# Gate rows on ScalarE and GpSimd, the output weight let go ahead of them, the binarized weight two steps later, in an adaLN Mamba-2 block

## The chip, the core and the metric

The kernel runs on one NeuronCore of a Trainium2 chip, in float32 throughout. The metric is the device time of one execution in microseconds (us), the median of several runs. The work is spread by hand over five engines: TensorE (PE in the profile: matmul and transpose; its weight loads are shown apart as PEld), VectorE (DVE), ScalarE (ACT), GpSimd (POOL) and SyncE (SP). SP does no arithmetic here, it issues transfers (DMAs). Each engine works through its own list of instructions strictly in order; an instruction that waits for another engine holds up everything behind it in its list. This is as true of SP's DMAs as of a matmul.

## The reference, cut to what matters

Four sequences of 512 tokens, 512 features each, go through two residual blocks. Six vectors per sequence, from one small product, shift, scale and gate them:

```python
mod = (silu(c) @ wmod).reshape(4, 6, 1, 512)
sa, ca, ga, sb, cb, gb = mod[:, 0] ... mod[:, 5]
ga = (2 * (ga >= 0) - 1) * maximum(abs(ga), 0.25)
gb = (2 * (gb >= 0) - 1) * maximum(abs(gb), 0.25)
h = layernorm(x) * (1 + ca) + sa
x = x + ga * mamba(h)          # in_proj, conv of 4 taps, silu, chunked scan, out_proj
h = layernorm(x) * (1 + cb) + sb
x = x + gb * (h @ bw.T + bias) # bw = sign(w) * mean(abs(w), row), 512 x 512
```

The Mamba part has 64 heads of width 16, 8 groups with state size 64, and chunks of 128 tokens. The change touches how `ga`, `gb` and `gb * bias` are made and when, and when `bw` is made.

## The kernel before, in words

**Tiles.** The 2048 tokens are cut into 8 halves `h` of 256 tokens, each into 2 chunks `c` of 128. A unit is one pair of the eight groups in one chunk, so a half has 8 units and the kernel 32, numbered u0, u1, ... here. Unit u is finished in step u by `stage2` (L630).

**A half's front.** `f_norm` (L307) normalizes the tokens on VectorE, with a power on GpSimd in it (`rs`, L298). `f_hT` (L335) turns them on TensorE (L330) and scales them on ScalarE (L347); its first columns are zeroed on GpSimd (L340). `f_dt` makes the step sizes, a long chain of small VectorE instructions (L371 to L404) that starts from the product `pa` (L368). `conv_pair` (L440) does two projections of 128 columns (`proj`, L434), and the convolution: one ScalarE instruction (L450) and three VectorE taps (L454) for each. A projection's PSUM bank is free when its last tap has read it; the pool `ps` has five such banks (tag "mm").

**A unit.** `stage0` (L570) has SP load the running sums that the decays come from (L541, L542) into one of two pairs of tiles, free when `py` of the unit two before has read it. ScalarE does 16 exponentials (L549), VectorE multiplies by the masked products (L625), TensorE forms `py` (L212, L215) and `stage2` gates it on VectorE and GpSimd.

**A chunk's tail.** `tail1` (L729) multiplies by the output weight `wout` (`po`, L739) and applies `gates`, `tail2` (L751) turns and modulates, `tail3` (L765) multiplies by the binarized weight `bwT` (`pf`, L775). For the first chunk they are in steps 4, 5 and 7.

**What is done once, in the first steps.** `load_late` (L181, step 0) loads the weights of four of the six vectors into places that are not yet in use: `wout`, `bwT`, two tiles of tag "z" and two thirds of `room`, the tile of tag "gates". `late_mods` (L233, step 1) multiplies them (`pg`), turns two of the rows for the second block, and makes the gates from the other two: five VectorE instructions (L256 to L260) on tiles of tags "h2" and "th", one load of the bias (L255) and three writes to DRAM (L262), all four on SP. `load_wout` (L264, step 2) can only load the 2 MB of the output weight when the products have read what lay there. `load_gates` (L717, step 3) reads the rows back, spread over 128 partitions. `signs(o)` (L269; two in step 2 and two in step 3) loads 128 rows of the second block's weight (L272), forms its row means (`alpha`, L274), signs (L277) and their product (L278, ScalarE). `turned_signs(o)` (L281; two in step 5, two in step 6) turns them on TensorE (L285) and puts them in `bwT` (L286).

**What sets the order.** The functions are called step by step, in each step those of the list `steps` (filled at L814 to L837) in the order of filling, then the unit's `burst`, `stage2`, `stage0` and `stage1`. A planner then fixes each engine's list before the run: by a model of times it takes what it holds to be ready, the earlier in the program first. Tiles of one tag share a fixed number of places ("h2" 2, "th" 2, "C" and "B" 3 each, "t" and "gates" 1): the first instruction that writes a tile waits until a place is free. `behind` (L781) puts a step's TensorE instructions behind the newest projection.

Of the kernel before, what the change touches and what calls it, by code (L numbers as in the profile page):

```python
# [11 lines left out]
F32 = mybir.dt.float32  # L12
AF = mybir.ActivationFunctionType
ALU = mybir.AluOpType
# [4 lines left out]
B, L, DM = 4, 512, 512  # L19
# [21 lines left out]
def adaln_mamba_block(  # L41
# [15 lines left out]
    nc = tc.nc  # L57
# [13 lines left out]
    wk = ctx.enter_context(tc.tile_pool(name="wk", bufs=2))  # L71
# [47 lines left out]
    gate_d = dram.tile([B, 3, DM], F32, name="gate_d")  # L119
# [25 lines left out]
    def load_wm_at(t6, place, k0=0):  # L145

        n = place.shape[1]
        nc.sync.dma_start(place, wm_v[:, k0 : k0 + n, t6 * DM : (t6 + 1) * DM])
        for k in range(n):
            wms[t6, k0 + k] = place[:, k]  # L150
# [27 lines left out]
    room = wk.tile([P, 3, DM], F32, tag="gates", name="wm3_g", bufs=1)  # L178
    room_z = wm_tiles(3, "z", 6, 2)

    def load_late(h):  # L181

        load_wm_at(2, wout[:, 0:NK])
        load_wm_at(5, wout[:, NK:])
        load_wm_at(4, bwT)
        for k in range(2):
            load_wm_at(3, room_z[k].unsqueeze(1), k)
        load_wm_at(3, room[:, 0:2, :], 2)


    sc = keep.tile([P, NK, 32], F32, name="sc")
# [17 lines left out]
    def glued(products, after=None):  # L209

        with tc.issue_after(after) if after else nullcontext():
            first = products[0]()  # L212
        with tc.issue_after(first.ins), tc.high_priority(offset=1000):
            for product in products[1:]:
                product()  # L215
# [17 lines left out]
    def late_mods(h):  # L233

        pg = ps.tile([P, DM], F32, tag="mm", name="pg")
        glued([
            partial(
                mm, pg[32 * j : 32 * j + 32, :], sc[:, k, :], wms[t6, k], start=(k == 0), stop=(k == NK - 1)
            )
            for k in range(NK) for j, t6 in enumerate((2, 5, 4, 3))  # L240
        ])
        row = wk.tile([P, DM], F32, tag="t", name="rows", bufs=1)
        nc.vector.tensor_copy(row, pg)
        pm = ps.tile([P, NK, P], F32, tag="mm", name="pm")
        for dt in range(NK):
            nc.tensor.transpose(pm[:, dt, :], row[:, dt * P : (dt + 1) * P], ident)
        nc.vector.tensor_copy(modT[:, 2], pm[:, :, 96 : 96 + B])
        nc.vector.tensor_scalar(modT[:, 3], pm[:, :, 64 : 64 + B], 1.0, None, ALU.add)

        g = row[0:64, :]  # L250
        sg = wk.tile([64, DM], F32, tag="h2", name="sg")
        ab = wk.tile([64, DM], F32, tag="h2", name="ab")
        brow = wk.tile([64, DM], F32, tag="th", name="brow")
        second = slice(32, 32 + B)
        nc.sync.dma_start(brow[second, :], ffn_b.partition_broadcast(B))  # L255
        nc.vector.tensor_scalar(sg, g, 0.0, 2.0, ALU.is_ge, ALU.mult)  # L256
        nc.vector.scalar_tensor_tensor(ab, g, -1.0, g, ALU.mult, ALU.max)
        nc.vector.tensor_scalar(ab, ab, 0.25, None, ALU.max)
        nc.vector.scalar_tensor_tensor(sg, sg, -1.0, ab, ALU.add, ALU.mult)
        nc.vector.tensor_mul(ab[second, :], sg[second, :], brow[second, :])  # L260
        for i, v in enumerate((sg[0:B, :], sg[second, :], ab[second, :])):
            nc.sync.dma_start(gate_d[:, i, :], v)  # L262

    def load_wout():  # L264
        nc.sync.dma_start(wout, w_outT.rearrange("(k p) e -> p k e", p=P))
# [548 lines left out]
    def at(step, f, *args):  # L814
        steps.setdefault(step, []).append((f, args))

    for h in range(NHALF):
        for step, f, args in (FIRST, SECOND)[h] if h < 2 else FRONT:
            at(max(0, h - 1) * NU + step, f, h, *args)
        if h % HPB == 0:  # L820
            at(h * NU + 3, load_gates, h // HPB)
        if h == 0:
            at(0, load_late, h)
            at(1, behind, 0, late_mods)
            at(2, load_wout)
            for o in range(NK):
                at(o // 2 + 2, signs, o)
    for o in range(NK):
        at(o // 2 + 5, behind, 1, turned_signs, o)
    for h in range(NHALF):  # L830
        for c in range(2):
            end = h * NU + (c + 1) * NP
# [7 lines left out]
    h = NHALF - 1  # L840
# [65 lines left out]
```

## Time and profile before

| what | value |
|---|---|
| median of 3 runs | 736.16 us (735.45 to 738.33) |
| the profiled execution | 737.38 us |
| its span, first to last instruction | 735.7 us |
| TensorE busy | 700.4 us, 95% of the span |
| VectorE busy | 599.5 us, 81% |
| ScalarE busy | 522.0 us, 71% |
| GpSimd busy | 254.8 us, 35% |
| TensorE clock granted, mean | 0.993 of full |

A busy share is a mean over the span. The chain of work that ended last is followed back from the last instruction, at each step to what released it. A timeline lists instructions of one engine with start and length; idle time stands in brackets with what ended it. A table of windows gives each engine's busy time in stretches of the span, with TensorE's granted clock, the share of the DMA engines and their rate.

### The profile page before, as it was taken

The numbers are of one execution on the slowest core, as the hardware profiler recorded it, in microseconds if no ns is written. First come the engines' busy times: TensorE is split into PE (matmuls) and PEld (weight loads), VectorE is DVE, ScalarE is ACT, GpSimd is POOL, SyncE is SP. The second block draws the span as 40 slices with busy tenths as digits, with TensorE's granted clock in tenths as the row PEclk, the third lists the DMA queues.
The fourth block names the chain that finished last, engine by engine and source line by source line (L and its number), as shares of the span: only waits on it lengthen the run. The fifth ranks groups of instructions, "written<-read, shape, count | busy, mean of one in ns | idle before, by whom it ended". The sixth has DMA issues, their size and how long they took to land.

```text
span 735.7 us, 15007 instructions
## 1 busy us (share of the span) xinstructions
PE 700.4 (95%) x5196; PEld 500.8 (68%) x5196; DVE 599.5 (81%) x1170; ACT 522.0 (71%) x1507; POOL 254.8 (35%) x297
## 2 busy tenths in 40 slices
PE   6999979899999999999999999999999999999997
PEld 3786746666677666677677666776667866677754
DVE  3869888876998678986899768996799867996995
ACT  2467658748696697785976787865968768788941
POOL 4021323444243332343223342433414332333652
PEclk9999989999999999999999999999999999999999
DMA  8991693535555256444644256552564537457720
GB/s 279 328 291 41 204 208 85 135 98 142 127 132 144 63 155 137 102 115 102 159 116 130 53 116 168 142 137 53 140 132 114 130 86 176 116 150 151 142 69 29
DMA packets 119067, 99.24 MB, mean 135 GB/s; under 512 B 73984, under 2 KB 97152, under 8 KB 118992
## 3 DMA queue, kind: packets, MB, share of 16 engines
q1 hardware_dynamic: 117808, 96.39, 52.3%
q0 software_dynamic: 896, 1.38, 0.7%
q8 instruction: 41, 0.67, 0.4%
q10 hardware_dynamic: 288, 0.52, 0.2%
q14 instruction: 34, 0.28, 0.1%
HBM read 92.47 MB, written 5.79 MB: 134 GB/s over the span
## 4 chain that ended last, share of the span: by engine, by line
PE 65%; ACT 16%; DVE 9%; DMA 4%; issue 4%; POOL 1%; SPq 1%; ACTq 0%; DVEq 0%; POOLq 0%
PE po L739 14%; PE pp_x L434 11%; PE pp_z L434 10%; ACT decay L549 9%; PE pp_C L434 7%; PE pp_B L434 5%; PE pf L775 3%; PE py L212 2%; PE py L215 2%; DVE decay L625 2%; ACT h L759 2%; DVE u_x L454 2%; DMA fw<-in_ffn_w 2%; ACT win L549 2%; PE gy L215 2%
## 5 line engine op out<-in xcount | busy, mean ns | idle before, releaser
L549 ACT ACTIVATE decay<-decay,st 128x128 f32<-128x128 f32 x960 | 293.9, 395 | 4.2 <-DMA decay<-sums_d 3.7
L625 DVE SCALAR_TENSOR_TENSOR decay<-decay,gm 128x1024 f32<-128x1024 f32 x120 | 160.8, 1341 | 50.3 <-ACT decay L549 47.2
L434 PE MATMUL pp_x<-hT,win 128*128 128x259 f32 x512 | 120.7, 390 | 7.3 <-DVE u_C L454 7.3
L434 PE MATMUL pp_z<-hT,win 128*128 128x256 f32 x512 | 118.1, 383 | 0.0
L434 PEld LDWEIGHTS pp_x<-hT,win 128*128 128x128 f32 x512 | 96.9, 193 | 25.2 <-ACT decay L549 7.7
L739 PE MATMUL po<-wout,z 128*128 128x512 f32 x256 | 113.8, 595 | 0.0
L434 PEld LDWEIGHTS pp_z<-hT,win 128*128 128x128 f32 x512 | 94.3, 189 | 16.3 <-issue 3.5
L675 POOL TENSOR_TENSOR z<-yt,z 128x256 f32<-128x256 f32 x62 | 62.9, 1015 | 76.1 <-DVE yt L674 57.8
L454 DVE SCALAR_TENSOR_TENSOR u_x<-pp_x,cw,u_x 128x256 f32<-128x256 f32 x192 | 83.6, 474 | 1.3 <-ACT u_x L450 0.7
L739 PEld LDWEIGHTS po<-wout,z 128*128 128x128 f32 x256 | 47.5, 190 | 53.1 <-issue 52.4
L672 POOL TENSOR_TENSOR yt<-yt,xs 128x256 f32<-128x256 f32 x46 | 41.4, 899 | 106.3 <-DVE yt L671 78.6
L507 POOL TENSOR_TENSOR xs<-u_x,rr 128x512 f32<-128x512 f32 x32 | 42.7, 1334 | 79.2 <-DVE u_x L459 61.3
L516 ACT ACTIVATE uz<-pp_z,zb 128x256 f32<-128x256 f32 x64 | 27.5, 470 | 59.0 <-PE pp_z L434 59.0
L215 PE MATMUL py<-decay,xpad 128*32 128x128 f32 x1680 | 66.3, 276 | 0.0
L434 PE MATMUL pp_B<-hT,win 128*128 128x259 f32 x256 | 63.5, 396 | 2.7 <-ACT decay L549 1.9
L434 PE MATMUL pp_C<-hT,win 128*128 128x259 f32 x256 | 59.6, 384 | 1.1 <-DVE u_x L454 1.1
L775 PE MATMUL pf<-bwT,h 128*128 128x512 f32 (+1 forms) x136 | 59.0, 578 | 1.4 <-ACT h L759 1.3
L434 PEld LDWEIGHTS pp_B<-hT,win 128*128 128x128 f32 x256 | 47.4, 193 | 14.5 <-ACT decay L549 3.1
L450 ACT ACTIVATE u_x<-pp_x,cb,cw 128x256 f32<-128x256 f32 x64 | 35.3, 560 | 30.5 <-PE pp_x L434 30.4
L434 PEld LDWEIGHTS pp_C<-hT,win 128*128 128x128 f32 x256 | 47.8, 189 | 9.4 <-PE pn L424 1.4
L679 POOL TENSOR_TENSOR xd<-xpad,st 128x256 f32<-128x256 f32 x48 | 34.1, 727 | 55.8 <-PE pst L215 28.3
L212 PE MATMUL py<-decay,xpad 128*32 128x128 f32 x240 | 47.4, 279 | 3.2 <-issue 2.2
(157 smaller groups left out, 1080.9 us busy)
## 6 DMA issues: line engine op xcount, KB each, us to landing
decay<-sums_d SPq DMA_DIRECT2D x120, 256.0 KB
decay<-sums_d SPq DMA_DIRECT2D x120, 128.0 KB
rr<-r_d SPq DMA_DIRECT2D x64, 128.0 KB
e<-e_d SPq DMA_DIRECT2D x96, 64.0 KB
win<-in_w_inT SPq DMA_DIRECT2D x4, 1024.0 KB
xr<-in_x SPq DMA_DIRECT2D x16, 256.0 KB
res<-o SPq DMA_DIRECT2D x15, 256.0 KB
x<-in_x SPq DMA_DIRECT2D x14, 256.0 KB
```

The source lines that it names most:

```text
L212: first = products[0]()
L215: product()
L434: last = mm(pm, win[:, k, col : col + P], H[h]["hT"][:, k, lo:], start=(k == 0), stop=(k == NK - 1))
L450: nc.scalar.activation(u[:, j, :], pm[:, KS - 1 :], AF.Identity, bias=cb[:, t : t + 1], scale=cw[:, t, KS - 1 : KS])
L454: nc.vector.scalar_tensor_tensor(u[:, j, :], pm[:, k : k + T], cw[:, t, k : k + 1], u[:, j, :], ALU.mult, ALU.add)
L507: nc.gpsimd.tensor_tensor(xs, xc, rr, ALU.mult)
L549: nc.scalar.activation(ets[r][:, i, :], ets[r][:, i, :], AF.Exp, bias=H[h]["st"][:, hd : hd + 1], scale=-1.0)
L625: nc.vector.scalar_tensor_tensor(ets[r], ets[r], 1.0, bc_mid(gm[:, r, :], HPG), ALU.min, ALU.mult)
L672: ew.tensor_add(t, t, xs)
L675: ew.tensor_mul(zg, t, zg)
L739: last_po = mm(po, H[h]["z"][g // 2][:, g % 2, c * CH : (c + 1) * CH], wout[:, g, :], start=(g == 0), stop=(g == NKI - 1))
L775: mm(pf, h2[:, k, :], bwT[:, k, cols], start=(k == 0), stop=(k == NK - 1))
```

## The change

The gates leave `late_mods` for a function of their own, `late_gates`, in step 2, after `load_wout` in the list of that step. It has one VectorE instruction (signs as +-0.5), one on ScalarE (the absolute value) and three on GpSimd; the three writes are issued by GpSimd instead of SP. Its three tiles are now the thirds of `room`, and the bias is loaded at the end of `load_late`, in step 0. `signs` moves from steps 2 and 3 to steps 4 and 5, `turned_signs` from steps 5 and 6 to 6 and 7. The arithmetic is the same: sign times 0.5 times 2 times the larger of the absolute value and 0.25.

```diff
@@ in load_late @@
         load_wm_at(3, room[:, 0:2, :], 2)
+        nc.sync.dma_start(brow[second, :], ffn_b.partition_broadcast(B))
@@ in late_mods @@
         nc.vector.tensor_scalar(modT[:, 3], pm[:, :, 64 : 64 + B], 1.0, None, ALU.add)
-
-        g = row[0:64, :]
-        sg = wk.tile([64, DM], F32, tag="h2", name="sg")
-        ab = wk.tile([64, DM], F32, tag="h2", name="ab")
-        brow = wk.tile([64, DM], F32, tag="th", name="brow")
-        second = slice(32, 32 + B)
-        nc.sync.dma_start(brow[second, :], ffn_b.partition_broadcast(B))
-        nc.vector.tensor_scalar(sg, g, 0.0, 2.0, ALU.is_ge, ALU.mult)
-        nc.vector.scalar_tensor_tensor(ab, g, -1.0, g, ALU.mult, ALU.max)
-        nc.vector.tensor_scalar(ab, ab, 0.25, None, ALU.max)
-        nc.vector.scalar_tensor_tensor(sg, sg, -1.0, ab, ALU.add, ALU.mult)
-        nc.vector.tensor_mul(ab[second, :], sg[second, :], brow[second, :])
+        late_row.append(row)
+
+    late_row = []
+
+    second = slice(32, 32 + B)
+    brow = room[0:64, 2, :]
+
+    def late_gates(h):
+        g = late_row.pop()[0:64, :]
+        sg, ab = room[0:64, 0, :], room[0:64, 1, :]
+
+        nc.vector.tensor_scalar(sg, g, 0.0, 0.5, ALU.is_ge, ALU.subtract)
+        nc.scalar.activation(ab, g, AF.Abs)
+        nc.gpsimd.tensor_scalar(ab, ab, 0.25, 2.0, ALU.max, ALU.mult)
+        nc.gpsimd.tensor_tensor(sg, sg, ab, ALU.mult)
+        nc.gpsimd.tensor_tensor(ab[second, :], sg[second, :], brow[second, :], ALU.mult)
         for i, v in enumerate((sg[0:B, :], sg[second, :], ab[second, :])):
-            nc.sync.dma_start(gate_d[:, i, :], v)
+            nc.gpsimd.dma_start(gate_d[:, i, :], v)
@@ the list of steps @@
             at(2, load_wout)
+            at(2, late_gates, h)
             for o in range(NK):
-                at(o // 2 + 2, signs, o)
+                at(o // 2 + 4, signs, o)
     for o in range(NK):
-        at(o // 2 + 5, behind, 1, turned_signs, o)
+        at(o // 2 + 6, behind, 1, turned_signs, o)
```

## The prediction

> **What bounds the kernel now.** I read the page's busy times first:
>
> ```profile
> PE 700.4 (95%) x5196; PEld 500.8 (68%) x5196; DVE 599.5 (81%) x1170; ACT 522.0 (71%) x1507; POOL 254.8 (35%) x297
> ```
>
> TensorE is the bound over the whole span, so a change to the first steps can only pay where TensorE stands idle or slow there. The table of windows says where (columns: stretch, length, then busy time and count of PE, PEld, DVE, ACT, POOL, then granted clock, DMA share, GB/s):
>
> ```profile
> 88.00:92.00 4.00, 4.00 (x20) 3.31 (x18) 4.00 (x11) 1.62 (x4) 1.34 (x3) 1.00 1.06 356
> 92.00:96.00 4.00, 1.93 (x42) 1.26 (x40) 2.51 (x7) 1.09 (x2) 2.96 (x5) 1.00 1.11 175
> 96.00:100.00 4.00, 0.59 (x2) 0.53 (x3) 3.68 (x10) 3.20 (x9) 0.00 (x0) 0.71 1.06 287
> 100.00:104.00 4.00, 4.00 (x11) 3.14 (x10) 4.00 (x10) 1.80 (x5) 0.45 (x1) 0.50 1.09 246
> ```
>
> From 94 to 99.4 TensorE is idle, and then "busy" at half clock with 11 matmuls. TensorE's timeline prices both:
>
> ```profile
> 88.56 3.67 PE L434 MATMUL pp_x<-hT,win 128*128 128x259 f32 x16
> 99.41 6.23 PE L434 MATMUL pp_x<-hT,win 128*128 128x259 f32 x16 [5.36 <-DVE u_C L454]
> ```
>
> The same 16 matmuls take 3.67 us before the gap and 6.23 after it. The gap costs 5.36 + (6.23 - 3.67) = 7.92 us. It waits for taps of `u_C` on VectorE, because the five PSUM banks hold two `pp_C`, two `pp_x` and one `pst`. VectorE's timeline says why the taps are late:
>
> ```profile
> 93.17 0.47 DVE L454 SCALAR_TENSOR_TENSOR u_C<-pp_C,cw,u_C 128x256 f32<-128x256 f32 x1
> 95.13 0.69 DVE L274 TENSOR_REDUCE alpha<-fw 128x1 f32<-128x512 f32 x1 [1.49 <-DMA fw<-in_ffn_w]
> ...
> 96.46 0.69 DVE L274 TENSOR_REDUCE alpha<-fw 128x1 f32<-128x512 f32 x1 [0.32 <-DMA fw<-in_ffn_w]
> ...
> 98.00 1.65 DVE L454 SCALAR_TENSOR_TENSOR u_C<-pp_C,cw,u_C 128x256 f32<-128x256 f32 x4
> ```
>
> Two `alpha` stand in VectorE's list ahead of the taps and wait for `fw`. Why `fw` is late is in SP's timeline:
>
> ```profile
> 67.49 0.29 SPq L255 DMA_DIRECT2D brow<-in_ffn_b  x1
> 72.66 0.60 SPq L262 DMA_DIRECT2D gate_d<-sg  x2
> 73.35 0.49 SPq L541 DMA_DIRECT2D decay<-sums_d  x1
> 77.66 0.24 SPq L262 DMA_DIRECT2D gate_d<-ab  x1
> ...
> 81.79 0.41 SPq L265 DMA_DIRECT2D wout<-in_w_outT  x1
> 82.26 1.44 SPq L272 DMA_DIRECT2D fw<-in_ffn_w  x2
> ```
>
> `fw` is issued right behind the 2 MB of `wout`, and `wout` behind the gate rows. In SP's waits the three are 10.9 us (L255, for the place of tag "th"), 4.8 (L262, for `sg`) and 3.7 (L262, for `ab`). The chain of waits runs through all of it, `ab` at 76.64, then SP, then 13.38 us of DMA to 96.44:
>
> ```profile
> 76.62 0.02 issue
> 76.64 1.00 DVE ab L260
> ...
> 82.26 0.76 SPq L272
> 83.02 0.04 issue
> 83.06 13.38 DMA fw<-in_ffn_w
> ```
>
> **What the Trainium skill says.** (1) "TensorE: Matmul & The Clock Gate", Part 1: the array's clock is halved after an idle window of about 3.4 us and comes back after about as long of work. The trace agrees: 5.36 us of idle gave a granted clock of 0.50, while the 1.93 us gap at 130.5 left it at 1.00. So a gap cut below 3 us also gives the slow matmuls back. (2) "SBUF — State Buffer", on the shared port pair: GpSimd and a VectorE instruction in a two-port mode or with two SBUF inputs exclude each other for a whole instruction. The trace fits: the normalization L300 took 1.50 us with GpSimd's L507 beside it, 0.55 as its median. (3) "GPSIMD Engine Reference", 1 and 3.1: each GpSimd core owns 16 partitions, so 64 partitions cost what 128 do; it prices a one-input operation at best at 1.8 cycles an element, and two inputs at 2.6.
>
> **The change, part by part.**
>
> *Stall at 94.* Without the two `alpha` and `sw`, VectorE goes from the tap ending at 93.64 to `B` (its `th_B` is done at 93.91, `B` takes 0.69) and two taps of 0.40 each: 95.4. TensorE restarts near 95.5, idle 1.45 us instead of 5.36: 3.9 us. The clock stays up: 2.56 us. Sum **-6.5**; at most -7.9. What is late next: `u_C` of the second bank and `u_x`, 9 taps of 0.40, while TensorE does 3.67 us of `pp_x1`: just covered. Then `po`, which began at 106.6, needs `z` of u3, from `yt` at 103.05, which moves with the taps; and `wout`.
>
> *SP.* Four issues leave SP's path here (the bias moves to step 0, about 43 us, behind loads; three writes go to GpSimd). SP's `wout` needs the `pg` products, done at 68.7, and the list ahead of it: decays of u3 (four issues of 0.6, free since `py` of u1 at 64.1) and two `rr`. I expect it near 70 to 72 instead of 81.8. At the 300 GB/s of this stretch 2 MB are 7 us, so it lands by 80, and nothing waits for it until `po` at 100: free. The decays of u3 come 6 to 9 us earlier; their exponentials (2 x 2.45 us on ScalarE) and products (2 x 1.2 on VectorE) leave the busy stretch 81 to 90. That can take the remaining 1.45 us of idle; but the same exponentials, if placed at 71.5 to 76.4, push `hT` from 77.25 by up to 1.9. I take **0** for the two, ends -1.4 and +1.9.
>
> *Gates.* VectorE loses L256 to L260, 0.42 + 0.68 + 0.41 + 0.67 + 0.99 = 3.17, and gains one of 0.42. Of these about 1.3 stood ahead of `rs_a` (71.13), the start of half 1. But GpSimd's `xd` runs until 71.69, so `rs_a` gains little there: **-0.5**, ends -1.3 and 0. The absolute value on ScalarE: no row for 64x512; 0.63 from the tanh of 128x512, in ScalarE's idle 3.2 us at 71.5: 0, at worst +0.6. GpSimd: `tensor_tensor` 128x512 is 1.28 (L745); by (3) the same for 64; the one-input one lies between 512 x 1.8 / 1.2 GHz = 0.77 (the page's price) and 1.51; I take 1.28. Three are 3.84, three issues at 0.6 (L389, L393, L407: 0.53 to 0.77) are 1.8: 5.6 us. GpSimd idles 8.0 us from 77.1 waiting for `rr`, and `rr` now comes earlier; it has 19 us between 71 and 90 for 7.5 + 5.6. What is behind them in its list: `xs`, the memset L340 that `pp_B` needs, `xd`; and the writes can starve no one, since the gates are read back at 95. I take **+0.5** for port sharing and a late memset; ends 0 and +3.
>
> *Signs.* `alpha` and `sw` (4 x (0.68 + 0.42) on VectorE, 4 x 0.72 on ScalarE) stay, but four of eight VectorE instructions go from 95 into 105 to 130, and the other four from 108 to 115 to after that. VectorE is full in 120 to 130 (10.0 of 10.0), and TensorE loses 0.8 + 1.9 us there to it already. Against it, `C` of half 1 (L459) had to wait for a place of tag "C" held by `sw0` until 121.66; it now goes at about 100. I take **+0.7**; ends -1 and +3. Their four loads go on SP in steps 4 and 5: 4 x 0.6, SP then waits for `py` anyway: 0.
>
> *Turning.* The last two stand behind `pp_x` of step 7 and ahead of `pf` (141.5), with 2 x 0.5 us of transposes and two ScalarE copies of 0.58 in between. Unless `pp_z` is put there, TensorE waits 1 to 2 us: **+0.3**, ends 0 and +2.
>
> Sum: -6.5 + 0 - 0.5 + 0.5 + 0.7 + 0.3 = **-5.5**. After 145 us TensorE is 98% busy and the half repeats, so the shift is carried to the end. The profiled execution has a span of 735.7 and 737.38 in all; 735.7 - 5.5 = 730.2, with 1.7 around it 731.9. It was 1.2 above the median 736.16; against that: 730.7.
>
> **Rivals.**
>
> 1. *Given back on VectorE.* The stall goes, but VectorE is the real bound from 80 to 140 (busy 8.0 to 10.0 of each 10 us from 80 on), and `alpha` moved to 105 to 130 comes out of TensorE there. For it: the full stretch. Against: VectorE still idles 6.5 us between 93 and 137 (1.49, 0.32, 1.70, 0.76, 0.76, 0.42, 1.03 in its timeline). A pair takes 1.02 from start to end (95.13 to 96.15), so the rest of the gain is -6.5 + 4 x 1.02 = -2.4: 733.8.
>
> 2. *GpSimd first.* The three operations and writes stand ahead of `rs_a`. The absolute value ends at 71.5 + 0.6, plus 5.6: `rs_a` at 77.8 instead of 71.8, TensorE idle 6.0 and 2.6 of slow clock, against the 6.5 won, less 0.5: 737.8. Against it: `f_norm` is of step 1, `late_gates` of step 2, and `rs_a` is ready first.
>
> 3. *Slower: SP stuck behind `fw`.* The loads of `fw2`, `fw3` need the two places of tag "h2" back, so `sw0`, `sw1` done; `sw0` needs a place of tag "C". Before, `alpha` ran at 107.97 and its `sw` only at 114.45, right after the products `gy` of step 4: that wait is real. If the planner gives `sw0` the place free only after step 6's `gy` (128), SP holds back the decays of u7 (issued at 121.1) by 7.8 us, over the 3.4 us that halve the clock: 7.8 + 2.6, less 5.5: 741. It decides from a wait of SP on `sw` longer than 6 us. Against it: step 4's `gy` frees a place first.
>
> 4. *Nothing moves:* the planner goes by readiness, and may again put `fw` behind `wout` and `alpha` ahead of the taps. As `wout` is issued 10 us earlier, `fw` is there by 82 and the wait is gone anyway; only if `wout` too stays behind other loads is little left: 735.
>
> **How the numbers follow.** Forecast 0.62, rivals 0.18, 0.07, 0.08, 0.05. About 0.5% (3.7 us) is what a measurement tells from no change. Of the forecast 0.59 lies under 732.5, of rival 1 0.07: faster 0.66. Rival 3 with 0.06, rival 2 with 0.02 lie over 739.8: slower 0.08. The rest, 0.26, is the same. The range runs from 726.5 (all of 7.9 and 1.8 of the upstream ends) to 736.0; below lie 0.04, above 0.13 (rivals 2 and 3 but for 0.02).
>
> **What would show it.** Right: TensorE's gap before `pp_x1` under 2 us and its 16 matmuls at 3.7; `wout` issued before 74; no SP wait on L262; `po` begins near 100. Wrong: a gap over 3 us anywhere in 70 to 145; `rs_a` later than 72.5; `alpha` waiting for its load; TensorE idle more than 2 us before `pf`; more than 4 us idle of TensorE in 105 to 140.

## The result, and the profile after

The change made the kernel slower: 742.86 us median of 8 runs (739.14 to 745.12) beside 735.94 (734.18 to 738.33), a ratio of 1.0088 with a 95% interval of 1.0066 to 1.0110. The forecast was 730.7 with a range up to 736.0. The profiled execution of the changed kernel took 743.53 us with a span of 741.8. Line numbers behind the gates are nine higher in the changed kernel: the taps are L463, `hT` L356, the exponentials L558, `alpha` L283, `pf` L784.

The page's busy times hardly move:

```profile
PE 703.4 (95%) x5196; PEld 502.8 (68%) x5196; DVE 597.0 (80%) x1166; ACT 522.1 (70%) x1508; POOL 262.2 (35%) x303
```

TensorE has the same 5196 instructions and 3.0 us more of busy time, and the span is 6.1 us longer: there is more idle time, and more time at half clock. Three marks on TensorE's timeline cut the span where both kernels do the same work: the first `pa` of half 1, the first `po` and the second `po`.

| profiled span | start to `pa` | `pa` to first `po` | first to second `po` | rest | sum |
|---|---|---|---|---|---|
| before | 77.87 | 28.75 | 47.73 | 581.35 | 735.7 |
| after | 75.96 | 30.61 | 53.05 | 582.18 | 741.8 |
| forecast, difference | -0.5 | -6.0 | +1.0 | 0 | -5.5 |
| measured, difference | -1.9 | +1.9 | +5.3 | +0.8 | +6.1 |

The loss is in two stretches. TensorE's timeline of the changed kernel shows the waits in them (start, length, then the idle time before it and what ended it):

```profile
75.96 0.44 PE L377 MATMUL pa<-hT,win 128*64 128x128 f32 x4 [1.24 <-ACT hT L356]
78.75 0.69 PE L377 MATMUL pa<-hT,win 128*64 128x128 f32 x4 [1.28 <-ACT hT L356]
102.03 3.55 PE L443 MATMUL pp_x<-hT,win 128*128 128x259 f32 x8 [3.69 <-DVE u_C L463]
121.73 0.63 PE L766 MATMUL ph<-ident,t 128*128 128x128 f32 x4 [2.09 <-DVE t L309]
135.85 5.46 PE L443 MATMUL pp_x<-hT,win 128*128 128x259 f32 x16 [3.68 <-ACT xpad L502]
```

The gap before `pp_x` at 94 to 99 is still there, 3.69 us long and ended by taps of the same tile, although no `alpha` stands ahead of them any more. The gap before `ph` at 120 is new. The one of 1.93 us that stood before `pp_x` at 130.5 has grown to 3.68 us, and its matmuls have become slow (5.46 us instead of 3.75). Upstream everything went as hoped. SP's timeline:

```profile
63.07 0.49 SPq L550 DMA_DIRECT2D decay<-sums_d  x1
...
65.97 0.59 SPq L551 DMA_DIRECT2D decay<-sums_d  x1
66.66 1.27 SPq L511 DMA_DIRECT2D rr<-r_d  x2
68.04 0.39 SPq L274 DMA_DIRECT2D wout<-in_w_outT  x1
```

`wout` goes at 68.04 instead of 81.79, and the loads of u3's decays at 63 to 66 instead of 73 to 80. That second gain is the first loss. ScalarE's timeline of the changed kernel where half 1 begins:

```profile
75.35 0.56 ACT L356 ACTIVATE hT<-phT,modT 128x256 f32<-128x256 f32 x1
75.80 2.44 ACT L558 ACTIVATE decay<-decay,st 128x128 f32<-128x128 f32 x8
78.14 1.01 ACT L356 ACTIVATE hT<-phT,modT 128x256 f32<-128x256 f32 x2
79.03 2.45 ACT L558 ACTIVATE decay<-decay,st 128x128 f32<-128x128 f32 x8
81.37 0.57 ACT L356 ACTIVATE hT<-phT,modT 128x256 f32<-128x256 f32 x1
```

Before, the four `hT` were one piece with u3's exponentials behind it:

```profile
77.25 1.93 ACT L347 ACTIVATE hT<-phT,modT 128x256 f32<-128x256 f32 x4 [0.70 <-PE phT L330]
...
81.46 2.45 ACT L549 ACTIVATE decay<-decay,st 128x128 f32<-128x128 f32 x8
```

Now those exponentials are ready, and two blocks of eight lie between the four. The fourth `hT` ends at 81.9 instead of 79.2, the last `pa` at 86.2 instead of 80.5, so VectorE's long chain for the step sizes starts late, VectorE is mostly idle until 88 and then has the taps in arrears.

The second loss looks in the trace to be of the same kind; e6 and e18 show below that this is only a part of it. ScalarE's timeline between the two `po`:

```profile
124.17 0.72 ACT L287 ACTIVATE sw<-sw,alpha 128x512 f32<-128x512 f32 x1 [4.49 <-DVE sw L286]
...
130.83 3.60 ACT L558 ACTIVATE decay<-decay,st 128x128 f32<-128x128 f32 x12
134.34 1.00 ACT L459 ACTIVATE u_C<-pp_C,cb,cw 128x256 f32<-128x256 f32 x2
135.23 0.57 ACT L502 COPY xpad<-pt_xt 128x512 f32<-128x512 f32 x1
```

ScalarE first waits 4.49 us for a moved `sw`, in a stretch in which it had been busy throughout. The window of the kernel before (stretch, length, busy times of PE, PEld, DVE, ACT, POOL, then granted clock, DMA share, GB/s) has both VectorE and ScalarE at 10.00:

```profile
120.00:130.00 10.00, 9.22 (x110) 7.14 (x111) 10.00 (x15) 10.00 (x32) 6.97 (x8) 1.00 0.46 110
```

And then the first instruction of the convolution and `xpad`, for which TensorE waits, stand behind 12 exponentials.

### The profile page after: what moved, and what is told of

Read it like the earlier page. It is cut to its first block, busy times and chain, and to the rows that moved or that the text cites. A ratio compares the mean times of both kernels' runs of the same rounds, so it can differ in the third digit from the quotient of the medians.

```text
span 741.8 us, 15015 instructions
## 1 busy us (share of the span) xinstructions
PE 703.4 (95%) x5196; PEld 502.8 (68%) x5196; DVE 597.0 (80%) x1166; ACT 522.1 (70%) x1508; POOL 262.2 (35%) x303
## 4 chain that ended last, share of the span: by engine, by line
PE 62%; ACT 20%; DVE 10%; issue 4%; DMA 3%; POOL 1%; ACTq 0%; SPq 0%; DVEq 0%; POOLq 0%
PE po L748 13%; ACT decay L558 11%; PE pp_x L443 10%; PE pp_z L443 10%; PE pp_C L443 7%; PE pp_B L443 5%; PE pf L784 4%; DVE decay L634 3%; PE py L216 2%; PE py L213 2%; ACT h L768 2%; DVE u_x L463 2%; ACT win L558 2%; DMA decay<-sums_d 2%; PE gy L216 2%
## 5 line engine op out<-in xcount | busy, mean ns | idle before, releaser
L558 ACT ACTIVATE decay<-decay,st 128x128 f32<-128x128 f32 x960 | 294.1, 395 | 6.1 <-DMA decay<-sums_d 5.7
L463 DVE SCALAR_TENSOR_TENSOR u_x<-pp_x,cw,u_x 128x256 f32<-128x256 f32 x192 | 84.6, 476 | 1.0 <-ACT u_x L459 0.2
L681 POOL TENSOR_TENSOR yt<-yt,xs 128x256 f32<-128x256 f32 x46 | 39.1, 850 | 117.2 <-DVE yt L680 77.5
L784 PE MATMUL pf<-bwT,h 128*128 128x512 f32 (+1 forms) x136 | 59.0, 578 | 1.3 <-ACT h L768 1.3
```

The source lines that it names most:

```text
L463: nc.vector.scalar_tensor_tensor(u[:, j, :], pm[:, k : k + T], cw[:, t, k : k + 1], u[:, j, :], ALU.mult, ALU.add)
L558: nc.scalar.activation(ets[r][:, i, :], ets[r][:, i, :], AF.Exp, bias=H[h]["st"][:, hd : hd + 1], scale=-1.0)
L681: ew.tensor_add(t, t, xs)
L784: mm(pf, h2[:, k, :], bwT[:, k, cols], start=(k == 0), stop=(k == NK - 1))
```

## The experiments

All have three rounds; a ratio is to runs of the kernel before beside it. This table gathers them; what is expected and what follows stands under each. The four stretches are those of one profiled span each.

| kernel | start to `pa` | `pa` to `po` | `po` to `po` | rest | median us | ratio (95%) |
|---|---|---|---|---|---|---|
| before | 77.87 | 28.75 | 47.73 | 581.35 | 735.94 | 1 |
| after | 75.96 | 30.61 | 53.05 | 582.18 | 742.86 | 1.0088 (1.0066 to 1.0110) |
| e1 gates part alone | 76.58 | 31.38 | 51.92 | 581.52 | 741.89 | 1.0077 (1.0060 to 1.0094) |
| e2 signs part alone | 77.70 | 23.92 | 54.57 | 581.41 | 738.97 | 1.0030 (1.0019 to 1.0042) |
| e3 after, `hT` first | 77.21 | 24.59 | 56.68 | 581.42 | 742.92 | 1.0094 (1.0078 to 1.0111) |
| e4 after, `sw` product on GpSimd | 75.72 | 27.93 | 52.92 | 582.63 | 740.75 | 1.0070 (1.0048 to 1.0091) |
| e5 before, `fw` ahead of `wout` | 77.58 | 24.80 | 47.87 | 581.25 | 733.66 | 0.9959 (0.9944 to 0.9974) |
| e6 after, exponentials last | 76.10 | 24.24 | 52.32 | 582.14 | 736.30 | 0.9999 (0.9989 to 1.0009) |
| e7 e2, `pf` a step later | 77.62 | 24.70 | 52.98 | 581.30 | 737.61 | 1.0014 (1.0003 to 1.0026) |
| e8 e2, signs behind the norm | 78.16 | 23.92 | 55.40 | 581.52 | 740.68 | 1.0042 (1.0023 to 1.0060) |
| e9 e1, exponentials last | 75.69 | 27.74 | 46.09 | 582.28 | 733.02 | 0.9945 (0.9924 to 0.9966) |
| e10 e5, exponentials last | 74.41 | 26.45 | 45.98 | 582.26 | 731.14 | 0.9924 (0.9903 to 0.9945) |
| e11 before, exponentials last | 74.50 | 28.35 | 46.73 | 581.72 | 731.99 | 0.9938 (0.9915 to 0.9961) |
| e12 e2, exponentials last | 74.07 | 25.80 | 50.08 | 582.05 | 731.53 | 0.9916 (0.9888 to 0.9945) |
| e13 e2, signs off VectorE | 76.43 | 23.18 | 54.45 | 581.94 | 739.18 | 1.0037 (1.0013 to 1.0061) |
| e14 after, signs off VectorE | 75.93 | 27.85 | 51.27 | 581.95 | 740.80 | 1.0078 (1.0049 to 1.0107) |
| e15 before, signs off VectorE | 77.64 | 27.18 | 47.12 | 581.56 | 733.39 | 0.9956 (0.9943 to 0.9969) |
| e16 turning alone late | 76.52 | 28.41 | 52.57 | 581.30 | 739.40 | 1.0048 (1.0026 to 1.0070) |
| e17 signs late, turning not | 76.73 | 24.76 | 52.27 | 581.24 | 734.56 | 0.9989 (0.9976 to 1.0002) |
| e18 e6, turning not late | 74.79 | 24.24 | 49.33 | 583.54 | 733.29 | 0.9959 (0.9947 to 0.9971) |

The first stretch differs by up to 1.7 us between kernels that do the same work up to there (76.43 in e13, 78.16 in e8), so only the second and third are read closely.

### The two parts, and the two suspected places

**e1: the gates' part alone** (the changed kernel with the steps of the signs as before).

```diff
-                at(o // 2 + 4, signs, o)
+                at(o // 2 + 2, signs, o)
...
-        at(o // 2 + 6, behind, 1, turned_signs, o)
+        at(o // 2 + 5, behind, 1, turned_signs, o)
```

> The changed kernel with the signs and their turning back in steps 2, 3 and 5, 6: only the gates' part of the change is left. Theory (two losses: half 1's hT stands behind u3's exponentials on ScalarE, some 5 us, which eats what the gates' part won; and ScalarE waits for sw in 119 to 124, another 5 us, which comes with the moved signs): the second loss goes, the first stays, so 737 us (735 to 739). Rival (the moved signs are harmless, GpSimd's operations and its shared port are the loss): 742 us or more, since the gates' part is all there and two alpha are back in front of the taps.

741.89, just under the rival's 742; but the rival's reason is wrong, as e9 shows below. The gates' part costs 5.3 us alone. `hT` is split here as in the changed kernel, and the stretch from `pa` to `po` is the longest of all, 31.38. The theory that the second loss comes only with the moved signs fell: from `po` to `po` it takes 51.92, 4.2 us more than before, with the signs in their old steps. TensorE's longest wait there:

```profile
143.35 3.28 PE L443 MATMUL pp_x<-hT,win 128*128 128x259 f32 x8 [2.79 <-ACT decay L558]
```

The trace puts its end down to the exponentials on ScalarE; a tap of `u_x` on VectorE ended within 0.03 us of them.

**e2: the signs' part alone** (the kernel before with signs two steps and turned signs one step later, the reverse of the diff above on it).

> The kernel before with only the signs and their turning two steps later, gates untouched. Theory: hT keeps its place ahead of u3's exponentials, the gap of 5.4 us at 94 and its slow matmuls go (-6.5), but a wait of ScalarE for sw in 115 to 130 costs up to 5: 734 us (731 to 736). Rival 1 (the gates' part is the whole loss): 729.5 us. Rival 2 (VectorE is the bound from 80 to 140, nothing can be won there): 736 to 738 us.

738.97, just over what the second rival says. The stretch from `pa` to `po` is 4.8 us shorter, by the mechanism of the forecast: the gap falls to 1.91 us, though the matmuls stay slow.

```profile
95.79 5.42 PE L434 MATMUL pp_x<-hT,win 128*128 128x259 f32 x16 [1.91 <-DVE u_C L454]
```

But from `po` to `po` it takes 6.8 us longer.

**e3: `hT` first**, its place in the list moved from step 2 to step 1.

```diff
-        (0, load_x, ()), (1, f_norm, ()), (2, f_hT, ()), (2, f_dt, ()),
+        (0, load_x, ()), (1, f_norm, ()), (1, f_hT, ()), (2, f_dt, ()),
```

> The changed kernel with f_hT of half 1 called in step 1 instead of 2, which puts its four ScalarE instructions ahead of u3's 16 exponentials. Theory: pa ends near 78 instead of 86, TensorE's waits for hT (2.5 us) and the slow clock after them go, the step-size chain starts 5 to 7 us earlier, po of the first chunk begins near 101 instead of 106.6; the second loss stays: 737 us (735 to 739). Rival (VectorE's sum of work is the bound, hT's place doesn't matter): within 1 us of the changed kernel, 742 to 743.

742.92. TensorE's timeline has all of `pa` in one piece:

```profile
77.21 1.10 PE L377 MATMUL pa<-hT,win 128*64 128x128 f32 x16
```

From there to `po` it takes 24.59 us instead of 30.61: the split `hT`, with the half clock behind it, does cost this stretch 6 us. The time is the rival's all the same, since from `po` to `po` it is now 56.68, 3.6 us more than in the changed kernel, with waits of 2.53 us before `ph` and 2.93 before `pf`. Mending the first loss did not mend the second.

**e4: the product of signs and means on GpSimd**, to free ScalarE of its wait for `sw`.

```diff
-        nc.scalar.activation(sw, sw, AF.Identity, scale=alpha)
+        nc.gpsimd.tensor_scalar(sw, sw, alpha, None, ALU.mult)
```

> The changed kernel with the product of sw and alpha (four instructions) on GpSimd instead of ScalarE, so that no exponential stands behind one. Theory: ScalarE's idle 4.5 us at 119.7 goes, and with it most of the second loss (5 us): 738.5 us (737 to 740.5). Rival (the loss after 107 is VectorE's, by alpha and sw in a full stretch, or GpSimd's port): 742 to 744 us, as VectorE's list is the same and GpSimd has four instructions more.

740.75, between the two. From `po` to `po` it is 52.92, as good as unchanged, so ScalarE's wait for `sw` costs nothing by itself. What is 2.7 us shorter is the stretch ahead of it, where the edit does nothing; the windows under e14 show what that is.

### The forecast's mechanism with nothing else moved

**e5: the kernel before, with the list of step 2 in another order**: the loads of `fw` stand ahead of `wout`, and nothing moves to another step.

```diff
-            at(2, load_wout)
             for o in range(NK):
                 at(o // 2 + 2, signs, o)
+            at(2, load_wout)
```

> The kernel before with the first two loads of the binarized weight issued ahead of the 2 MB of the output weight instead of behind it; nothing else. It measures the stall alone: alpha no longer waits (1.8 us of VectorE), but stays in front of the taps. Theory (the stall is worth what the forecast said, and it was lost elsewhere): TensorE's gap at 94 falls from 5.4 to 2 to 3.5 us, with or without the slow matmuls after it: 733 us (731.5 to 735). Rival (whatever is won before the first po is lost again until the second po, as in the three kernels where po came 3 to 5 us earlier): 736 us, po of the first chunk earlier, po of the second not.

733.66, the theory. SP's timeline and TensorE's:

```profile
81.44 0.95 SPq L272 DMA_DIRECT2D fw<-in_ffn_w  x2
82.44 0.43 SPq L265 DMA_DIRECT2D wout<-in_w_outT  x1
```

```profile
97.64 3.74 PE L434 MATMUL pp_x<-hT,win 128*128 128x259 f32 x16 [1.81 <-ACT decay L549]
```

Two loads that change places on SP make the `alpha` run at 87.40 and 89.46 instead of 95.13 and 96.46, the gap 1.81 us instead of 5.36 and its 16 matmuls 3.74 us instead of 6.23. Two shorter gaps come ahead of it (1.02 and 0.96), so 4.0 us are won up to `po`. From `po` to `po` it takes 47.87, as before: the win is carried to the end where the later lists stay.

### The exponentials

**e6: the changed kernel, the exponentials of halves 0 and 1 last** in what the planner chooses from.

```diff
-        for r in range(2):
-            for i in range(HPG):
+        for r, i in [(r, i) for r in range(2) for i in range(HPG)]:
+            with tc.high_priority(offset=-150) if h < 2 else nullcontext():
```

> The changed kernel with the exponentials of halves 0 and 1 traced at a lower priority (150 places later), so that the planner puts ScalarE's copies out of PSUM and hT ahead of them. Theory (the changed kernel loses because exponentials, ready earlier in the plan, stand ahead of what TensorE waits for: hT at 75, xpad at 135): both of these waits go, 735 us (733 to 738). Rival (VectorE's list with alpha in it makes the loss): the waits move to decay on VectorE and the time stays at 741 to 744.

736.3: 6.6 us less than the changed kernel, `hT` in one piece, and 24.24 us from `pa` to `po`. The theory's number, but not yet its proof: the control is e11. And the gain lies in the first stretch alone. From `po` to `po` it still takes 52.32 instead of 53.05: the wait for `xpad` is gone, but TensorE now waits 2.89 us before `ph` and 1.91 before `py`, both for VectorE. So the exponentials are not what makes most of the second loss in the changed kernel.

**e9, e10, e11, e12: the same edit** on the gates' part alone (e1), on e5, on the kernel before, and on the signs' part alone (e2).

> The gates' part alone (signs and turned_signs in their steps of before) with the exponentials of halves 0 and 1 last in the planner's choice. Theory (the gates' part costs its 5 us only through u3's exponentials that it lets go early, which stand among the instructions of half 1's front): the 5.3 us of the gates' part alone are gone and some of the stall at 94 is won, 733 to 736, half 1's hT in one piece or ahead of the exponentials, and the gap before pp_x of half 1 under 3 us. Rival (the gates on GpSimd cost by themselves, through GpSimd's list ahead of the memset and port sharing): 739 to 742 as without the edit.

> The kernel before with fw loaded ahead of wout, and the exponentials last as well. Theory (with fw early there is nothing left in this stretch that the exponentials hold up, since SP lets the decays of u3 go as late as before): no further gain, 732.5 to 735. Rival (exponentials cost wherever the planner puts them): 729 to 731.

> The kernel before with the exponentials of halves 0 and 1 last, nothing else: the control for the same edit on the changed kernel, where it won 6.6 us. Theory (the exponentials stand in the way only where the change lets them go early): within 1.5 us of before, 734.5 to 737.5. Rival (the edit is a gain on any kernel of this family and says nothing on the change): 729 to 731.5.

> The kernel before with signs and turned_signs two and one steps later (which alone gave 739.0), and the exponentials last. Theory (part of the moved signs' loss is the copies of bwT and the convolution's first instruction behind blocks of exponentials on ScalarE): 734 to 736.5, no wait before pf over 1 us. Rival (the loss is VectorE's alpha and sw between po and ph alone): 738 to 740.

The control went against the theory: 731.99. The edit is a gain of 0.62% on the kernel before, about 4.3 us, so most of the 6.6 us of e6 says nothing on the change. What remains of the theory is what the edit wins beyond that. On the gates' part alone it is 1.0077 to 0.9945, 1.3%, twice as much: the whole cost of the gates' part is gone (733.02 beside the control's 731.99, with intervals that overlap), and both its stretches come down to the control's or below: 31.38 to 27.74 from `pa` to `po` (control 28.35), 51.92 to 46.09 from `po` to `po` (control 46.73). `hT` is in one piece again:

```profile
75.07 1.94 ACT L356 ACTIVATE hT<-phT,modT 128x256 f32<-128x256 f32 x4
```

For the gates' part the place of the exponentials is the cause, and not its operations on GpSimd or port sharing, which e9 keeps. The stall at 94 stays in e9, 5.17 us, where its theory had under 3. On the signs' part it is 1.1%, and the rest of their loss from `po` to `po` (50.08 beside 46.73) is met by what they win ahead of it (25.80 beside 28.35); 731.53 is faster than both its theory and its rival had. e10 is at 731.14, nearer the rival: `fw` ahead of `wout` adds nothing that can be told once the exponentials are last.

### The stretch from `po` to `po`

**e7: e2 with `pf` one step later.**

```diff
-            late = {(0, 0): (0, 1, 3), (NHALF - 1, 0): (2,),
+            late = {(0, 0): (0, 1, 4), (NHALF - 1, 0): (2,),
```

> Only the signs moved (as in e2_signs_only), and pf of the first chunk one step later, in step 8, so that it stands behind pp_z and no longer waits for the last two copies of the turned weight. Theory: the wait of 1.6 us before pf and some of the 2.5 around it go: 736.5 us (735 to 738). Rival (TensorE finds another late producer in their place, the copies still stand behind 16 exponentials): 738.5 to 740.

737.61, about 1.2 us of e2's loss by the ratios and inside the theory's range, in its slower half; the wait for `bwT` before `pf` is gone, and 0.52 us of it is back before the `pp_z` that now stands there.

**e8: e2 with all four `signs` in step 5, on VectorE behind the normalization of the first chunk.**

```diff
-        nc.vector.tensor_reduce(alpha, fw, AX.X, ALU.add, apply_absolute_value=True)
+        with tc.issue_after(newest["norm"]):
+            nc.vector.tensor_reduce(alpha, fw, AX.X, ALU.add, apply_absolute_value=True)
...
-                at(o // 2 + 4, signs, o)
+                at(5, signs, o)
```

> Only the signs moved, but all four in step 5 and on VectorE behind the first chunk's normalization (L300), so that no alpha stands between po and ph. Theory: TensorE's wait of 2.7 us before ph and the slow matmuls behind it (1.5 us) go: 735.5 us (733.5 to 738). Rival (VectorE and ScalarE have no room in 105 to 145, the work comes out of TensorE elsewhere): 738 to 740.

740.68, on the rival's side and 0.7 above its range. The wait before `ph` falls only from 2.72 to 1.69 us, and others grow.

**e13, e14, e15: the signs' work taken off VectorE**, on e2, on the changed kernel and on the kernel before as the control. The three leave the signs out and take most of the row out of its mean, so they do less work and make another result; they serve only to place the cost.

```diff
-        nc.vector.tensor_reduce(alpha, fw, AX.X, ...
+        nc.vector.tensor_reduce(alpha, fw[:, 0:16], AX.X, ...
...
-        nc.vector.tensor_scalar(sw, fw, 0.0, 0.5, ALU.is_ge, ALU.subtract)
-        nc.scalar.activation(sw, sw, AF.Identity, scale=alpha)
+        nc.scalar.activation(sw, fw, AF.Identity, scale=alpha)
```

> Signs and turned_signs alone in their late steps (739.0 before this edit), with the row means taken over 16 of 512 columns and sw made by ScalarE straight from fw: the signs and most of the means are left out, so VectorE has four tiny instructions in place of 4.4 us, and ScalarE, SP and TensorE issue what they did. Theory (what the moved signs cost is VectorE's 4.4 us in the stretch between the first and the second po, half of it ahead of the normalization): from first to second po 48 to 50 us instead of 54.6, and 732 to 734.5. Rival (it is ScalarE's copies behind exponentials and the turning ahead of pf): 52.5 us or more, 736.5 to 739.

> The changed kernel with the same work left out (row means over 16 columns, no signs). Theory: its first po stays near 106 (that loss is the split hT), the interval to the second falls from 53.05 to 48 to 50, and 738 to 740. Rival (the interval is ScalarE's and TensorE's): 742 or more.

> The control: the kernel before with the same work left out. VectorE still waits for fw at 93 to 96, as the tiny row means stand where the whole ones did; theory: the stall at 94 shrinks by the work only, about 1 to 2 us of 5.36, 733.5 to 735.5, and the interval from first to second po stays within 1 us of 47.7. Rival (VectorE's work for the signs costs the same anywhere): 731 to 733.

e13 is at 739.18 and 54.45 us from `po` to `po`, as good as e2's 54.57: VectorE's 4.4 us are not what the moved signs cost, and that theory fell. Its TensorE waits twice for copies of `bwT` on ScalarE:

```profile
132.55 0.66 PE L467 MATMUL pt_bt<-ident,B 128*128 128x128 f32 x4 [1.87 <-ACT bwT L286]
...
141.95 3.70 PE L775 MATMUL pf<-bwT,h 128*128 128x512 f32 x8 [1.58 <-ACT bwT L286]
```

e14 (740.8; 51.27) takes 1.8 us off that stretch of the changed kernel, between its theory and its rival; as a whole it can't be told from the changed kernel (1.0078 beside 1.0088). e15 wins 1.6 us at the stall and 0.6 behind it, as expected; its 733.39 is 0.1 below the theory's range.

e14 shows another thing. Its start of half 1 is that of the changed kernel, with the same split `hT` and the same two gaps, 1.25 and 1.28 us. The windows of the changed kernel, 76 to 84 (stretch, then busy times of PE, PEld, DVE, ACT, POOL, then the granted clock):

```profile
76.00:80.00 4.00, 2.72 (x14) 1.63 (x14) 2.35 (x2) 4.00 (x14) 3.93 (x7) 0.74 0.19 60
80.00:84.00 4.00, 4.00 (x13) 2.56 (x12) 1.39 (x1) 1.94 (x7) 4.00 (x4) 0.50 0.00 0
```

and those of e14:

```profile
76.00:80.00 4.00, 2.72 (x18) 1.50 (x18) 2.32 (x2) 4.00 (x14) 3.93 (x7) 1.00 0.14 42
80.00:84.00 4.00, 4.00 (x23) 3.05 (x20) 1.70 (x2) 2.18 (x7) 4.00 (x4) 1.00 0.00 0
```

The same two gaps halved the clock in one and not in the other, 13 matmuls in 4 us beside 23, and the last `pa` ends at 86.16 and 83.36. These 2.8 us are the whole difference between the two from `pa` to `po` (30.61 and 27.85). e4 (27.93) kept full clock there too, which is what made it shorter. e13 shows the same at the stall: its gap is that of e2, 1.91 us before the same `pp_x`, and its matmuls are not slow.

```profile
94.52 3.75 PE L434 MATMUL pp_x<-hT,win 128*128 128x259 f32 x16 [1.91 <-DVE u_C L454]
```

**e16: the turned signs alone one step later.**

```diff
-        at(o // 2 + 5, behind, 1, turned_signs, o)
+        at(o // 2 + 6, behind, 1, turned_signs, o)
```

> The kernel before with turned_signs alone one step later, signs where they were. Theory (the turning ahead of pf costs 1 to 2 us, as the later pf of e7 won 1.4): 737 to 738.5, TensorE waiting for bwT before pf. Rival (the turning costs only where the signs are late too): 735.5 to 736.7.

739.4, more than the theory had. ScalarE's timeline and TensorE's:

```profile
139.72 2.44 ACT L549 ACTIVATE decay<-decay,st 128x128 f32<-128x128 f32 x8
142.06 0.62 ACT L458 ACTIVATE th_x<-u_x 128x512 f32<-128x512 f32 x1
142.58 1.06 ACT L286 ACTIVATE bwT<-pbw 128x512 f32<-128x512 f32 x2
```

```profile
143.70 5.40 PE L775 MATMUL pf<-bwT,h 128*128 128x512 f32 x8 [2.76 <-ACT bwT L286]
```

The transposes themselves are done at 139.9. Their two copies stand behind a block of eight exponentials and are ready at 143.6; `pf` waits 2.76 us and then takes 5.40 us instead of 3.59. That is 4.6 us at one place.

**e17: the signs late, the turned signs not**, and **e18: the same on e6**.

```diff
-        at(o // 2 + 6, behind, 1, turned_signs, o)
+        at(o // 2 + 5, behind, 1, turned_signs, o)
```

> Signs alone two steps later (steps 4 and 5), turned_signs where it was (steps 5 and 6). Theory (the moved signs give their win at 94 back through the turning one step later, whose last two copies of bwT stand behind a block of 8 exponentials ahead of pf): the 5.3 us gap before pp_x is gone, pf does not wait, first to second po 48 to 50.5 us, and 732.5 to 735. Rival (alpha and sw between po and the normalization cost their 5 to 7 us by themselves): 737 to 739.

> The changed kernel with the exponentials last (736.3 before this edit) and turned_signs back in steps 5 and 6. Theory (with these two edits both losses of the change are taken away, and the shorter stall at 94 is left): first to second po 47 to 49.5 us instead of 52.3, 731 to 733. Rival (the two parts of the change hinder each other elsewhere, as each alone with the exponentials last was at 731.5 to 733 and both at 736.3): 735 to 737.

e17 is at 734.56, the theory's time, and `pf` doesn't wait. Its stretch from `po` to `po` is not the theory's: 52.27 in the profiled span, which is one of the four longest of twelve (735.0, clock 0.995; eight others have 732.3 to 733.6 at 0.998). There too TensorE stands idle, 2.32 us before `pp_x`, and ScalarE is in a block of exponentials meanwhile. TensorE's timeline:

```profile
131.10 5.43 PE L434 MATMUL pp_x<-hT,win 128*128 128x259 f32 x16 [2.32 <-ACT decay L549]
```

ScalarE's:

```profile
128.54 2.44 ACT L549 ACTIVATE decay<-decay,st 128x128 f32<-128x128 f32 x8
130.88 0.57 ACT L493 COPY xpad<-pt_xt 128x512 f32<-128x512 f32 x1
```

The trace puts the end of the wait down to that block (130.98); a tap of `u_C` on VectorE ended at 130.96, and in the kernel before it was such a tap that `pp_x` waited for here. Which of the two it was is not shown. `xpad`, which ended at 131.45, it was not.

e18 falls from 736.3 to 733.29, 0.3 above its theory's range, and from 52.32 to 49.33 from `po` to `po`: with the exponentials last too, the later turning is worth 3 us. TensorE's timeline keeps these two gaps; the first leaves the matmuls at full clock:

```profile
94.33 3.75 PE L443 MATMUL pp_x<-hT,win 128*128 128x259 f32 x16 [2.83 <-DVE u_C L463]
...
116.04 0.66 PE L766 MATMUL ph<-ident,t 128*128 128x128 f32 x4 [2.19 <-DVE t L309]
```

So the changed kernel with both edits is faster than the kernel before, but not than the control with the exponentials last (e11, 731.99): what it wins at 94 (24.24 beside 28.35) it gives back between the two `po` (49.33 beside 46.73) and after.

**The fastest** are e10, e11 and e12, 731 to 732 us with intervals that overlap. None has the change's gates; e9, which has them, can't be told from e11.

## Why the prediction was wrong, point by point

The step that failed is the one called SP: it took the earlier decays of u3 as free, with +1.9 us at worst. The change brought u3's exponentials into the middle of `hT`, and the stretch from `pa` to `po`, forecast 6.0 us shorter, became 1.9 us longer. The terms Signs and Turning, +1.0 together, were too small as well: the next stretch became 5.3 us longer. With the exponentials last, 3.0 us of that go with the later turning (e18 beside e6). Two of the prediction's own signs of being wrong came: gaps of TensorE over 3 us (3.69 and 3.68), and more than 4 us of its idle time in 105 to 140 (2.09 and 3.68).

- **Stall at 94, -6.5.** The mechanism is shown: with the late `alpha` out of the way the gap falls from 5.36 to 1.9 us, and `pa` to `po` is 4.8 (e2), 4.0 (e17) and 4.0 us (e5) shorter. The size was too large. Three taps, not two, stand between `B` and TensorE's restart, 0.4 us; and the slow matmuls stayed in e2 (5.42 us after 1.91 us of idle). In the changed kernel itself the gain was lost to the next point.
- **SP, 0 with ends -1.4 and +1.9.** The step named the exponentials of u3 and said that they would push `hT` if placed at 71.5 to 76.4. They were placed between the four `hT`, two blocks of 2.45 us. Without the slow clock at `hT` the stretch is then 27.85 (e14) instead of 23.2 to 24.6 (e2, e3, e13), 3 to 5 us more, and 2.8 us more where the clock was halved. e9 shows it from the other side: with the exponentials last the gates' part costs nothing that can be measured. That "nothing waits for it until `po`" was true of `wout`; the decays that SP issues behind the same writes were the ones that mattered. The 4.2 us that the gates' part alone loses between the two `po` (e1) were in no term.
- **"A gap cut below 3 us also gives the slow matmuls back."** Wrong. 1.91 us in e2 and the pair of 1.24 and 1.28 in the changed kernel were followed by half clock; 1.91 us in e13, 1.81 in e5 and the same pair in e14 were not. "TensorE: Matmul & The Clock Gate", Part 1, of the Trainium skill also says that the window is free-running and does not reset when a kernel starts. So two equal gaps can lie differently in it, but no run here shows that this is what parted them, and half clock after gaps much shorter than the page's idle window is not in its table. Here the measurement decides: a gap of 2 us has to be priced with the slow clock as a risk, not as safe.
- **Gates, 0.** As far as e9 can tell, right as a whole; its parts were not. `rs_a` took 0.70 us from 69.00 instead of 2.55 from 71.79, so it was done 4.6 us earlier, and `pa` 1.9 us, better than the -0.5. GpSimd's three operations took 1.94, 1.27 and 2.13 us and the three issues 1.84, 7.2 us in all instead of 5.6. The late memset was a misreading: the one at 79.93 zeroes columns of half 2, those of half 1 were copied at 16.32 (L351), and `pp_B` ran at 76.33 without it.
- **Signs, +0.7, and Turning, +0.3 with ends 0 and +2.** These failed in size and in place. Turning alone costs 4.8 us between the two `po` (e16), at the very wait that the step named, because it set two copies of 0.58 us where a block of eight exponentials came first. Signs alone cost 4.5 us there in the profiled span of e17, but as a whole e17 is 0.11% faster than before, and that is no difference that can be told. The price was looked for on VectorE, from its full windows; e13 shows that it isn't there. For the turning it is on ScalarE, which had the same 10.00 in that line; for the signs alone it is not settled. In the changed kernel itself `pf` (147.51) doesn't wait, and its losses lie at `ph` and `pp_x`; no run takes the turning alone back from it, so its share there is not measured.
- **"After 145 us the shift is carried to the end"**: right within 0.8 us in the changed kernel, 2.2 us off in e18.
- **The rivals.** The third, SP behind `fw`, didn't happen: SP waits at most 3.0 us for `sw`. Nor did the second, since `rs_a` came earlier. The first, given back on VectorE, has the right shape in e2 (won at 94, lost at 105 to 145) on the wrong engine. That the change could be slower through ScalarE's list had no price beyond the +1.9.

Open: e6 beside e9 and e12, where each part alone is level with the control and both together are 4.3 us behind it; e18 takes 3 of these away by the turning, and the rest is not explained. Every edit makes the planner order all lists anew, so no run changes one thing only. Why the exponentials last win 4 us on the kernel before was not tried apart; 3.4 us of it lie ahead of `pa`, of which up to 1.7 may be the spread of that stretch. There the trace of e11 has `rs_a` done at 70.0 instead of 74.3.

## What to carry to other kernels

Where a planner or a list in fixed order places the work, price a change of readiness as well as of work: here what became ready earlier was placed earlier, and a block of it landed in the middle of what the bound engine waited for next. When a step is moved, ask of every instruction of it what will stand ahead of it in its engine's list at the new place; two copies of 0.6 us out of PSUM behind a block of eight exponentials were a wait of 2.76 us for TensorE (e16). And try the smallest edit that removes the shown wait first: two loads exchanged on one queue (e5) gave a gain where the whole change gave a loss.

## What the runs showed of the hardware that was not expected

- At idle gaps of 1.2 to 2.9 us the length doesn't tell whether the half clock follows. A gap of 1.91 us before the same `pp_x` was followed by it in e2, e7, e8 and e17 (5.42 to 5.43 us for the 16 matmuls) and not in e13 (3.75). It came after 2.76 (e16), 2.32 us (e17) and the pair of 1.24 and 1.28 (after), and not after 1.81 (e5), 1.93 (before, at 130.5), 2.83 (e18) or the pair of 1.25 and 1.28 (e14).
- The changed kernel's eight spans follow their mean granted clock: 737.4 us at 0.995, 739.5 at 0.993, 740.7 to 743.4 at 0.986 to 0.988.
- On GpSimd a `tensor_tensor` of 64 x 512 took 1.27 us in the changed kernel, as one of 128 x 512 did (1.28), so half the partitions cost the same. The same 64 x 512 took 2.29 us in e9, and one of 4 x 512 took 2.13 and 1.78. Each of the longer ones ran beside an instruction of VectorE with two inputs, and VectorE's `z` beside the one of 2.13 took 1.64 us instead of 0.68.
- The power `rs_a` of half 1 on GpSimd took 2.55 us in all nine kernels with the old gates and the exponentials in their old order, and 0.70 in the other eleven. In the kernel before, VectorE's L259 and L625 ran beside it, 0.67 and 1.21 us. Both this and the point above fit what the prediction says in (2).
